# Fixing the order of the first period's loads, and regrouping the last block's output projection, in a time-mix and GELU-FFN kernel

## The chip, the cores and the metric

The kernel runs on one core of a Trainium2 chip. The metric is the device time of one execution in microseconds (us); where several runs are compared, it is their median.

## What is computed

The input x has 4 sequences of 1024 tokens with 512 channels, in float32. The reference normalizes every token over its channels and adds two branches to x:

```python
xn = _layernorm(x, axis=-1)
x = x + attn(xn) + ffn(xn)

# attn: time mix with the token before, recurrence over the tokens
xx = concatenate([x[:, 1:2, :], x[:, :-1, :]], axis=1) - x
k = einsum('btc,hc->bth', x + xx * time_mix_k, Wk)      # 704 hidden
r = einsum('btc,hc->bth', x + xx * time_mix_r, Wr)
w = exp(-exp(time_decay))
state = state * w + relu(k_t);  out_t = state * r_t     # scan over t
out = layernorm(einsum('bth,ch->btc', out, Wv)) * ln_gamma + ln_beta

# ffn: 512 -> 2048 -> 512
D = gelu(x.astype(float16) @ W0.T + bias0).astype(float16)
E = (D @ W1.T + bias1).astype(float16)
```

## The kernel before

**Blocks and periods.** The tokens are cut into 8 blocks of 512 (two for each sequence; `LAST` is 7). A block has 4 token tiles `s` of 128. The channels are 4 chunks `c` of 128, the hidden width 704 is five full tiles `h` and a half one, and the 2048 FFN units are 16 chunks `n` of 128. The main loop (L741) has one period for each block `i`, and in it one step for each FFN chunk `n` (L833).

**A step.** It issues, in this order: `up` (L654) of the chunk `AHEAD` = 2 further on, eight matmuls `pd` from W0 and the float16-rounded x; the `followers`, which are the VectorE and ScalarE work left over from the projection matmuls of the step before; the GELU of `up`'s result (L669, and a cast at L674); `down` (L679) of chunk `n`, eight matmuls for each step into four accumulators `pe`, one for each token tile; the step's entry in `pieces`, if it has one, which is a group of matmuls of the time mix (hidden tiles of k and r at the start of the period, output projection `po` at its end); and the step's list `bg[n]` of other work (loads, weight splits, normalization and transposes of the next block).

**Weights in two or three parts.** W0 and W1 are kept as high and low parts, so that their products are exact enough: `split` (L159) makes the high part on ScalarE (L160) and the low one on VectorE (L161) from a raw load. W0 stays in SBUF; its raw loads are `load_w0(g, c)` (L168), where `g` is the group of four FFN chunks that need it, and `split_w0` (L172) splits one of them. W1 is loaded raw (`load_w1_raw`, L184), split in the first period, written to DRAM (`store_weights`, L180) and fetched from there in the later periods. The weights of k and r are used raw in block 0 and in three parts from block 1 on.

**The start.** `first_inputs` (L337) normalizes, transposes on TensorE (L377, `pt`) and mixes block 0. Its x tile (`load_x`, L95) lies in a buffer of which there is one; block 1's x (`x_next`, L715) goes to the same buffer, so it can be loaded only when the last of the transposes has read block 0's. After that, L702 to L717 issue 25 loads on SyncE's queue: W0's group 0, three chunks of W1, the remaining k and r weights, the half tiles, W0's group 1, block 1's x, W0's group 2. Then a block ordered by hand (L724 to L736) computes the first hidden tiles, splits W0's group 0, splits two chunks of W1 and half of W0's group 1, and does `up` of chunks 0 and 1. In ScalarE's order the splits of W0's (1,0) and (1,1) (L735) stand ahead of the GELU of chunk 0 (L736).

**What sets the order.** A scheduler lays out each engine's instructions. Inside `tc.manual_schedule(engines=...)` the engines named keep the order of the text; elsewhere the scheduler orders by its own estimate of when things are ready. The block at L724 names TensorE, VectorE, ScalarE and SyncE; so does the first period of the main loop. The later periods name TensorE and SyncE only, so there VectorE's, ScalarE's and GpSimd's orders are the scheduler's. The loads of L702 to L717 stand in no such block.

**The end.** In the last block the last four FFN chunks (`tail` = 4) have no `down` in the loop. Their `up` runs in steps 10 to 13. The output projection stands in steps 12 to 15, one token tile each: `out_piece` (L625) issues five float32 matmuls of a tile (L588); for an odd tile it also issues the half hidden tile of both tiles of the pair (L600), and leaves as follower the residual of the pair (`residual`, L608: statistics at L265, then L615, L620, L621). The residual of tiles 2 and 3 thus comes after the loop (L866). The closing block (L868 to L880) adds a bias to two accumulators (`base`, L873), does the sixteen remaining `down` products tile by tile, and for each result rounds (L641), adds (L647) and stores (L651). The PSUM pool `mm`, with four banks, holds `pd`, `po` and the last column sums; `pe` has four banks of its own.

Of the kernel before, what the change touches and what calls it, by code (L numbers as in the profile page):

```python
# [17 lines left out]
P = 128  # L18
# [4 lines left out]
def time_mix_and_gelu_ffn(  # L23
# [26 lines left out]
    nc = tc.nc  # L50
# [4 lines left out]
    NS = TB // P  # L55
    NC = C // P
# [6 lines left out]
    NF = HID // P  # L63
    H0 = NF * P
# [3 lines left out]
    LAST = len(blocks) - 1  # L68
# [10 lines left out]
    def part(name, dtype=F32R, tag="q", bufs=QS):  # L79
        return wide.tile([P, TB], dtype, tag=tag, name=name, bufs=bufs)  # L80
# [7 lines left out]
    def bank(name):  # L88
        return ps_mm.tile([P, TB], F32, tag="mm", name=name)

    def tokens_of(i, s):
        b, t0 = blocks[i]
        return b, slice(t0 + s * P, t0 + (s + 1) * P)

    def load_x(i, name, amid=lambda: None):  # L95
        xs = const.tile([P, NS, C], F32, tag="x", name=f"{name}_{i}")
        for s in range(NS):
            if s == NS // 2:
                amid()
            b, rows = tokens_of(i, s)  # L100
            nc.sync.dma_start(xs[:, s, :], x[b, rows, :])
        return xs


    FIRST = 3
    sources = (wkT, wrT)
    raw_w = {}

    def load_raw(kind, h):
        w = part(f"w{'kr'[kind]}_{h}", F32)  # L110
        raw_w[kind, h] = w.rearrange("p (c k) -> p c k", c=NC)
        src = sources[kind].rearrange("(c p) k -> p c k", p=P)
        nc.sync.dma_start(raw_w[kind, h], src[:, :, h * P : (h + 1) * P])
# [29 lines left out]
    raw_half = part("raw_half", F32).rearrange("p (two c k) -> p two c k", two=2, c=NC)  # L143
# [24 lines left out]
    def load_w0(g, c, **home):  # L168
        w0_raw[c, g] = raw = part(f"w0raw_{g}_{c}", F32, **home)
        nc.sync.dma_start(raw, w0T[c * P : (c + 1) * P, g * TB : (g + 1) * TB])  # L170
# [13 lines left out]
    def load_w1_raw(n):  # L184
        w1_raw[n] = part(f"w1raw_{n}", F32)
        nc.sync.dma_start(w1_raw[n], w1T[n * P : (n + 1) * P, :])
# [511 lines left out]
    AHEAD = 2  # L698
    state = {}
    behind = ExitStack()  # L700
    first_x16s, pks = first_inputs(x_now, behind)
    for c in range(NC):  # L702
        load_w0(0, c)
    for n in range(AHEAD + 1):
        load_w1_raw(n)
    for h in range(FIRST, NF):
        load_raw(0, h)
        load_raw(1, h)
    for kind, src in enumerate(sources):
        nc.sync.dma_start(  # L710
            raw_half[:, kind], src.rearrange("(c p) k -> p c k", p=P)[:, :, H0:]
        )
    for c in range(NC):
        load_w0(1, c)
    x_next = load_x(1, "x")  # L715
    for c in range(NC):
        load_w0(2, c)  # L717

    def several(fn, *calls):
        for args in calls:  # L720
# [2 lines left out]
    engines = {e.engine for e in (nc.tensor, nc.vector, nc.scalar, nc.sync)}  # L723
# [15 lines left out]
    followers = []  # L739
    e16s = []  # L740
    for i in range(len(blocks)):  # L741
        with tc.manual_schedule(
            engines=engines if i == 0 else {nc.tensor.engine, nc.sync.engine}
        ):
            j = i + 1
            tail = 4 if i == LAST else 0
            by_columns = range(NS // 2, NS) if tail else ()
            pieces, bg = {}, defaultdict(list)

            def put(n, fn, *args):  # L750
                bg[n].append(lambda: fn(*args))

            def fetch_kr(block, kind, h):
                if block == 1 and kind == 1:
                    ks[block, kind, h] = split_kr(kind, h)
                else:
                    ks[block, kind, h] = load_kr(block, kind, h)

            def fetch_x():
                state["x"] = load_x(j, "x")  # L760

            def fetch_residual():
                zs[i] = load_x(i, "xres")

            def stats(*ss):
                norm_stats(j, state["x"], *ss)

            def turn(first, end):
                transposed(state["x"], first, end)

            def fresh_mixed(c):
                mixed(j, c)

            for s in range(NS):
                pieces[12 + s] = [out_piece, i, s]
            if i == 0:
                state["x"] = x_next
                pieces[1] = [raw_k, i, 3]
                pieces[3] = [raw_r, i, 3]
                pieces[5] = [raw_k, i, 4]  # L780
                pieces[7] = [raw_r, i, 4]
                pieces[9] = [
                    lambda i: raw_halves(i, [bank(f"pkr_{i}_{q}") for q in range(2)]), i
                ]
                put(0, several, split_w0, (1, 2), (1, 3))
                for c in range(NC):
                    put(2 + c - (c == 0), split_w0, 2, c)
                    put(3 + c, load_w0, 3, c)
                    put(5 + c, split_w0, 3, c)
                put(1, stats, *range(NS))  # L790
                put(3, lambda: norm_apply(j, state["x"]))
                for h in range(NF):
                    put(1 + 2 * h, split_kr, 0, h)
                put(4, turn, 0, 1)
                put(5, turn, 1, 5)
                put(7, turn, 5, 10)
                put(8, turn, 10, 11)
                put(9, turn, 11, 16)
                put(4, load_late_constants)
                put(12, split_half)  # L800
                mix_at = (11, 12, 13, 15)
            else:
                order = [(0, h) for h in range(NF)] + [(1, h) for h in range(NF)]
                for k, (kind, h) in enumerate(order):
                    pieces[k + 2 * kind] = [three_pass, i, kind, h]
                    if k > 1:
                        put(k - 2 + 2 * (k > 6), fetch_kr, i, kind, h)
                pieces[5] = [half_pass, i, 0]
                pieces[6] = [half_pass, i, 1]
                put(2, split_xr, i, 0)  # L810
                put(4, split_xr, i, 1)
                put(5, split_xr, i, 2)
                put(5, split_xr, i, 3)
                if j <= LAST:
                    put(2, fetch_x)
                    put(4, stats, *range(NS))
                    put(5, lambda: norm_apply(j, state["x"]))
                    put(6, turn, 0, 2)
                    put(7, turn, 2, 6)
                    put(8, turn, 6, 10)  # L820
                    put(9, turn, 10, 14)
                    put(10, turn, 14, 16)
                mix_at = (11, 12, 13, 14)
            put(11 if j <= LAST else 2, fetch_residual)
            if j <= LAST:
                put(10, x16, j)
                for c, n in enumerate(mix_at):
                    put(n, fresh_mixed, c)
                put(13, fetch_kr, j, 0, 0)
                put(14, fetch_kr, j, 0, 1)  # L830

            pe = [ps_e.tile([P, C], F32, tag="pe", name=f"pe_{i}_{s}") for s in range(NS)]
            for n in range(NN):  # L833
                ahead = n + AHEAD
                if ahead == NN and j <= LAST:
                    xf = ffn_input(j)
                nxt = (i, ahead) if ahead < NN else (j, ahead - NN)
                gelu = up(*nxt) if nxt[0] <= LAST else None
                for follow in followers:
                    follow()  # L840
                followers = []
                if gelu:
                    d = gelu()
                if n < NN - tail:
                    operands = waiting.pop(0)
                    for s in range(NS):
                        down(n, s, *operands, end=NN - tail if s in by_columns else NN)
                if gelu and i > 0:
                    waiting.append((d, load_w1(*nxt)))
                for s in (2 * n, 2 * n + 1):  # L850
                    if s < len(e16s):
                        finish(i - 1, s, e16s[s])
                if n in pieces:
                    fn, *args = pieces[n]
                    followers.append(fn(*args))
                if i == 0 and ahead + 1 < NN:
                    load_w1_raw(ahead + 1)
                for fn in bg[n]:
                    fn()
                if i == 0:  # L860
                    waiting.append((d, load_w1(*nxt)))
                store_weights()
            if not tail:
                e16s = [rounded(i, s, pe[s]) for s in range(NS)]
# [59 lines left out]
```

## Time and profile before

| what | value |
|---|---|
| median of 3 runs | 904.9 us (904.3 to 905.19) |
| the profiled execution | 904.43 us, its span 902.6 us |
| TensorE matmuls busy | 888.0 us (98%), 3688 instructions |
| TensorE weight loads busy | 657.7 us (73%) |
| VectorE | 590.5 us (65%) |
| ScalarE | 349.7 us (39%) |
| GpSimd | 73.1 us (8%) |
| moved by DMA | 165.60 MB, mean 183 GB/s |
| mean granted TensorE clock | 0.994 |

The profile is one execution. The span runs from the first to the last instruction of the program, and the execution's time is 1.8 us longer. Busy shares are means over stages with different limits, so the page is to be read together with the chain of waits (what released each step, followed back from the end), the list of waits by engine, the timelines, and tables of busy time by stage. A line such as `PE pe L681 <- ACT d L674` says that TensorE's matmul at line 681, which writes `pe`, waited for ScalarE's instruction at line 674, which writes `d`. In these views PE is TensorE's matmuls, PEld its weight loads, DVE VectorE, ACT ScalarE, POOL GpSimd and SP SyncE; a `q` behind an engine's name means its instruction queue, which issues DMAs. Ends of matmuls are modelled, so distances between their starts are the safer measure.

### The profile page before, as it was taken

The numbers are of one execution on the slowest core, as the hardware profiler recorded it, in microseconds if no ns is written. First come the engines' busy times: TensorE is split into PE (matmuls) and PEld (weight loads), VectorE is DVE, ScalarE is ACT, GpSimd is POOL, SyncE is SP. The second block draws the span as 40 slices with busy tenths as digits, with TensorE's granted clock in tenths as the row PEclk, the third lists the DMA queues.
The fourth block names the chain that finished last, engine by engine and source line by source line (L and its number), as shares of the span: only waits on it lengthen the run. The fifth ranks groups of instructions, "written<-read, shape, count | busy, mean of one in ns | idle before, by whom it ended". The sixth has DMA issues, their size and how long they took to land.

```text
span 902.6 us, 10591 instructions
## 1 busy us (share of the span) xinstructions
PE 888.0 (98%) x3688; PEld 657.7 (73%) x3688; DVE 590.5 (65%) x989; ACT 349.7 (39%) x597; POOL 73.1 (8%) x142
## 2 busy tenths in 40 slices
PE   8999999999999999999999999999999999999996
PEld 8577658877588866888668885788767887588854
DVE  4577886886659558595575946678555775565126
ACT  4756533554144332344324442244333444144320
POOL 1100000100111001010111000010011100000001
PEclk8999999999999999999999999999999999999999
DMA  4969746644375642945448454485535654466621
GB/s 122 323 231 331 241 163 212 220 152 143 138 240 192 198 152 94 306 156 161 147 157 275 158 190 137 142 272 162 174 120 191 237 171 144 140 220 211 190 79 47
DMA packets 77888, 165.60 MB, mean 183 GB/s; under 512 B 9199, under 2 KB 15372, under 8 KB 77836
## 3 DMA queue, kind: packets, MB, share of 16 engines
q1 hardware_dynamic: 77776, 164.92, 55.0%
q8 instruction: 29, 0.48, 0.2%
q14 instruction: 23, 0.19, 0.1%
q10 hardware_dynamic: 60, 0.02, 0.0%
HBM read 140.26 MB, written 24.64 MB: 183 GB/s over the span
## 4 chain that ended last, share of the span: by engine, by line
PE 91%; DVE 4%; DMA 2%; SPq 1%; ACT 1%; issue 1%; POOL 0%; ACTq 0%; DVEq 0%
PE pd L659 24%; PE pe L681 24%; PE po L588 15%; PE pa L534 13%; PE pb L335 7%; PE ph L562 2%; PE po L600 2%; PE pk L335 2%; DMA w0raw<-in_L_ffn_W 1%; DVE xnT L291 1%; PE pr L335 1%; DMA x<-in_L_attn_x 0%; DMA wk<-in_L_attn_Wk 0%; PE pkr L509 0%; DVE xres L647 0%
## 5 line engine op out<-in xcount | busy, mean ns | idle before, releaser
L681 PE MATMUL pe<-w,d 128*128 128x512 f32 x1008 | 249.2, 389 | 2.2 <-ACT d L674 2.2
L681 PEld LDWEIGHTS pe<-w,d 128*128 128x128 f32 x1008 | 189.0, 188 | 43.0 <-ACT d L674 2.6
L659 PE MATMUL pd<-xf,w0h 128*128 128x512 f32 x512 | 209.5, 409 | 1.3 <-DVE y L547 0.8
L659 PE MATMUL pd<-xf,w0l 128*128 128x512 f32 x512 | 199.7, 390 | 0.0
L669 ACT ACTIVATE d<-pd,late_sb 128x512 f16<-128x512 f32 x128 | 87.6, 684 | 187.0 <-PE pd L659 186.7
L588 PE MATMUL po<-wv_sb,g 128*128 128x512 f32 x320 | 142.4, 592 | 0.0
L547 DVE SCALAR_TENSOR_TENSOR y<-pb,a 128x512 f32<-128x512 f32 x70 | 48.2, 689 | 141.8 <-PE pb L335 127.0
L659 PEld LDWEIGHTS pd<-xf,w0h 128*128 128x128 f32 x512 | 96.1, 188 | 38.0 <-issue 16.1
L659 PEld LDWEIGHTS pd<-xf,w0l 128*128 128x128 f32 x512 | 96.1, 188 | 23.8 <-issue 4.5
L588 PEld LDWEIGHTS po<-wv_sb,g 128*128 128x128 f32 x320 | 60.6, 189 | 64.9 <-issue 61.8
L546 ACT ACTIVATE a<-pa 128x512 f32<-128x512 f32 x70 | 41.7, 596 | 117.2 <-PE pa L534 117.2
L674 ACT CAST d<-d 128x512 fp32r<-128x512 f16 x128 | 79.4, 621 | 3.8
L291 DVE STREAM_TRANSPOSE xnT<-x 32x512 f32<-32x512 f32 x112 | 78.7, 702 | 1.8
L265 DVE BATCH_NORM_STATS2 sty<-po 128x6 f32<-128x512 f32 x32 | 21.9, 683 | 86.2 <-PE po L600 86.2
L534 PE MATMUL pa<-hk,kr 128*128 128x512 f32 x140 | 54.5, 389 | 0.0
L534 PE MATMUL pa<-lk,kr 128*128 128x512 f32 x140 | 54.5, 389 | 0.0
L259 POOL TENSOR_SCALAR ry<-mvy 128x1 f32<-128x1 f32 x32 | 15.2, 475 | 397.2 <-DVE mvy L266 397.2
L534 PE MATMUL pa<-hr,kr 128*128 128x512 f32 x120 | 46.7, 389 | 0.0
L534 PE MATMUL pa<-lr,kr 128*128 128x512 f32 x120 | 46.7, 389 | 0.0
L549 ACT ACTIVATE y<-y 128x512 f32<-128x512 f32 x35 | 22.2, 634 | 57.3 <-DVE y L547 57.3
L246 ACT CAST hk<-uk 128x512 fp32r<-128x512 f32 x28 | 17.4, 620 | 58.4 <-DVE uk L213 58.4
L335 PE MATMUL pb<-mk,kr 128*128 128x512 f32 x140 | 37.4, 389 | 0.0
(133 smaller groups left out, 1042.3 us busy)
## 6 DMA issues: line engine op xcount, KB each, us to landing
w<-w1d SPq DMA_DIRECT2D x110, 512.0 KB, 3.5
kr<-krd SPq DMA_DIRECT2D x195, 256.0 KB, 4.1
x<-in_L_attn_x SPq DMA_DIRECT2D x32, 256.0 KB, 4.9
w1d<-w SPq DMA_DIRECT2D x16, 512.0 KB, 3.0
xres<-in_L_attn_x SPq DMA_DIRECT2D x32, 256.0 KB, 4.4
krd<-wt SPq DMA_DIRECT2D x30, 256.0 KB, 3.5
out<-xres SPq DMA_DIRECT2D x28, 256.0 KB, 4.4
w0raw<-in_L_ffn_W SPq DMA_DIRECT2D x16, 256.0 KB, 5.7
```

Source lines behind the costliest of these rows:

```text
L265: nc.vector.bn_stats(st6, src)
L291: nc.vector.transpose(dst[i * Q : (i + 1) * Q, :, :, j, :], src[j * Q : (j + 1) * Q, :, :, i, :],)
L335: return nc.tensor.matmul(dst, w[:, c, :], src, start=(c == 0), stop=(c == NC - 1))
L534: nc.tensor.matmul(pa, w[p][:, c, :], xs[j, c][p], start=(c == 0 and p == 0), stop=(c == NC - 1 and p == 1),)
L546: nc.scalar.activation(a, pa, AF.Copy, scale=1.0 + 1.0 / S)
L547: nc.vector.scalar_tensor_tensor(y, pb, -1.0 / S, a, ALU.mult, ALU.add)
L549: nc.scalar.activation(y, y, AF.Relu)
L588: nc.tensor.matmul(pos[s], gs[i, h][:, s * P : (s + 1) * P], wv_sb[:, h, :], start=(h == 0), stop=False,)
L659: nc.tensor.matmul(pd, w0[c, g][p][:, k * P : (k + 1) * P], xf[c], start=(c == 0 and p == 0), stop=(c == NC - 1 and p == 1),)
L669: nc.scalar.activation(d16, pd, AF.Gelu, bias=b0_sb[:, n : n + 1])
L674: nc.scalar.copy(d, d16)
L681: nc.tensor.matmul(pe[s] if sum_ is None else sum_, d[:, s * P : (s + 1) * P], w1[p][:, cols], start=(n == first and p == 0), stop=(n == e ...
```

## The change

There are two edits. The 25 loads of L702 to L717 are put, in the same order of the text, into a block in which SyncE keeps that order. And the entries of `pieces` are keyed by step and place (`n, s`) instead of by step, so that a step can have up to four of them; in the last block the output projection of tiles 0 and 1 is put in step 12 and that of tiles 2 and 3 in step 13, where it was one tile each in steps 12 to 15. The other blocks keep one tile for each step, and all other entries keep their steps.

```diff
-    for c in range(NC):
-        load_w0(0, c)
-    for n in range(AHEAD + 1):
-        load_w1_raw(n)
...
-    for c in range(NC):
-        load_w0(1, c)
-    x_next = load_x(1, "x")
-    for c in range(NC):
-        load_w0(2, c)
+    with tc.manual_schedule(engines={nc.sync.engine}):
+        for c in range(NC):
+            load_w0(0, c)
+        for n in range(AHEAD + 1):
+            load_w1_raw(n)
+        for h in range(FIRST, NF):
+            load_raw(0, h)
+            load_raw(1, h)
+        for kind, src in enumerate(sources):
+            nc.sync.dma_start(
+                raw_half[:, kind], src.rearrange("(c p) k -> p c k", p=P)[:, :, H0:]
+            )
+        for c in range(NC):
+            load_w0(1, c)
+        x_next = load_x(1, "x")
+        for c in range(NC):
+            load_w0(2, c)
...
             for s in range(NS):
-                pieces[12 + s] = [out_piece, i, s]
+                pieces[12 + (s // 2 if i == LAST else s), s] = [out_piece, i, s]
...
-                if n in pieces:
-                    fn, *args = pieces[n]
-                    followers.append(fn(*args))
+                for s in range(NS):
+                    if (n, s) in pieces:
+                        fn, *args = pieces[n, s]
+                        followers.append(fn(*args))
```

More of the change, by code (lines that the diff above doesn't have):

```diff
@@ L701, in time_mix_and_gelu_ffn @@
     first_x16s, pks = first_inputs(x_now, behind)
-    for c in range(NC):
-        load_w0(0, c)
-    for n in range(AHEAD + 1):
-        load_w1_raw(n)
[L706 to L712, printed above, removed]
-    for c in range(NC):
-        load_w0(1, c)
-    x_next = load_x(1, "x")
-    for c in range(NC):
-        load_w0(2, c)
+    with tc.manual_schedule(engines={nc.sync.engine}):
[15 more added lines that the diff above has]
+            load_w0(2, c)
     def several(fn, *calls):
@@ L774, in time_mix_and_gelu_ffn @@
             for s in range(NS):
-                pieces[12 + s] = [out_piece, i, s]
+                pieces[12 + (s // 2 if i == LAST else s), s] = [out_piece, i, s]
             if i == 0:
                 state["x"] = x_next
[L778 to L782, printed above, removed]
+                pieces[1, 0] = [raw_k, i, 3]
+                pieces[3, 0] = [raw_r, i, 3]
+                pieces[5, 0] = [raw_k, i, 4]
+                pieces[7, 0] = [raw_r, i, 4]
+                pieces[9, 0] = [
                     lambda i: raw_halves(i, [bank(f"pkr_{i}_{q}") for q in range(2)]), i
@@ L804, in time_mix_and_gelu_ffn @@
                 for k, (kind, h) in enumerate(order):
-                    pieces[k + 2 * kind] = [three_pass, i, kind, h]
+                    pieces[k + 2 * kind, 0] = [three_pass, i, kind, h]
                     if k > 1:
                         put(k - 2 + 2 * (k > 6), fetch_kr, i, kind, h)
-                pieces[5] = [half_pass, i, 0]
-                pieces[6] = [half_pass, i, 1]
+                pieces[5, 0] = [half_pass, i, 0]
+                pieces[6, 0] = [half_pass, i, 1]
                 put(2, split_xr, i, 0)
```

## The prediction

> **What bounds the kernel now.** I read the page's busy shares first, then TensorE's waits, then the chain of waits for 19 to 47 us, SyncE's timeline at the start, the stages, and last the end of each engine's timeline.
>
> ```profile
> PE 888.0 (98%) x3688; PEld 657.7 (73%) x3688; DVE 590.5 (65%) x989; ACT 349.7 (39%) x597; POOL 73.1 (8%) x142
> ```
>
> TensorE (PE) is busy 888.0 of 902.6 us, so only its pauses, or the stretch after its last matmul, can give time back. Its waits (total, times, longest) are few:
>
> ```profile
> PE small L410 <- issue: 2.6, 1, 2.6
> PE pe L681 <- ACT d L674: 2.2, 1, 2.2
> PE pd L659 <- DVE y L547: 0.8, 1, 0.8
> PE idle L353 <- PEq L907: 0.8, 1, 0.8
> PE pd L659 <- DVE y L573: 0.5, 1, 0.5
> ```
>
> The 2.2 us wait, `down` of chunk 0 waiting for ScalarE's (ACT's) GELU output, is the one that the first edit can reach. Followed back in the chain (start, us, what):
>
> ```profile
> 20.37 0.45 PE pt L377 x4
> ...
> 20.84 0.34 SPq L101
> ...
> 24.07 6.25 DMA w0raw<-in_L_ffn_W
> ...
> 33.28 4.97 DMA w0raw<-in_L_ffn_W
> 38.25 0.02 issue
> 38.27 0.62 ACT w0h L160
> ...
> 38.91 0.62 ACT w0h L160
> ...
> 39.55 1.28 ACT L669
> ...
> 40.84 0.70 ACT d L669
> ...
> 41.56 0.63 ACT d L674
> ...
> 42.23 2.14 PE pe L681 x8
> ```
>
> The GELU stands in ACT's queue behind the splits of `w0raw(1,0)` and `(1,1)`, which landed at 38.25. These were late because SyncE (SP) issued block 1's x first, and x waits for its single buffer, free when block 0's last transposes (L377) are over:
>
> ```profile
> 7.27 1.48 SPq L113 DMA_DIRECT2D wr<-in_L_attn_Wr  x3
> 20.84 1.76 SPq L101 DMA_DIRECT2D x<-in_L_attn_x  x4
> 22.65 1.85 SPq L170 DMA_DIRECT2D w0raw<-in_L_ffn_W  x4
> ```
>
> From 8.75 to 20.84 SP issues nothing. The stage table has the DMA engines 22% busy at 61 GB/s in 9 to 21 us, then 98% at 306 GB/s in 21 to 45.
>
> At the end VectorE (DVE) decides, from the last projection tile on:
>
> ```profile
> 887.30 0.70 DVE L265 BATCH_NORM_STATS2 sty<-po 128x6 f32<-128x512 f32 x1 [4.14 <-PE po L600]
> 892.15 0.68 DVE L873 TENSOR_TENSOR base<-pe,b_sb 128x512 f32<-128x512 f32 x1
> 899.44 0.42 DVE L647 TENSOR_TENSOR xres<-xres,e 128x256 f32<-128x256 f32 x1
> ```
>
> DVE has no further pause from 887.30 to 899.86; the last stores land at 902.6. PE's last matmul starts at 894.68, inside that.
>
> **What the Trainium skill says.** "DMA: Bandwidth & Descriptors", section "Anatomy of one DMA": DMA engines wait for no semaphore, the issuing sequencer does, before dispatch. The trace agrees: one x load holds SP for 12.0 us and the independent loads behind it start late. "Perfetto Trace Analysis", section "Tensor Engine Instruction": ACT and DVE run strictly in order, and PE's end times are estimates. The first half is what the chain shows at 38.27 (the GELU's own input was complete near 36.4); for the second I count PE's loss from starts. "ScalarE: Activation LUTs", section "What ACT_TABLE_LOAD costs", has about 1283 ns for the load; the row at 39.55 has 1.28 us.
>
> **Part 1, SP's order.** Nothing is added or removed; all 25 loads of the text keep their sizes. What moves: four x loads (0.43 us of issue each) go behind 17 others: w0(0), three w1raw, four raw weights, two half weights, w0(1). No wait is added. Behind x's wait on SP there now stand only w0(2), first split at 47.75, and the loop's loads and stores.
>
> *When does w0(1,1) land?* A 262,144-byte load at 306 GB/s takes 0.857 us. w0(1,1) is the 15th load; the halves count half each, so 14 full ones. If w0(0,0) issues at 8.8 and lands in the 5.7 us of the issue table: 8.8 + 5.7 + 13 x 0.857 = 25.6 us. The other bound: the w0 buffers could be ones that the same transposes free, so that the trace would hide their wait behind x's. Then w0(0,0) starts at 20.84 and w0(1,0) gains only x's four places: 38.25 - 4 x 0.857 = 34.8; (1,1) at about 35.5. I take the early one; it hardly matters, as follows.
>
> *What is late next?* ACT runs without a pause to the end of the w1 splits (31.57 + 1.22 = 32.79). Early bound: two splits to 34.05, table load to 35.35; then chunk 0's `up` is the later (last matmul near 36.04, over near 36.4), so GELU 36.55 to 37.25 and cast to 37.87. Late bound: splits to 36.15, table load to 37.45, GELU to 38.15, cast to 38.8. PE wants it when `up` of chunk 2 is through: last start 39.67 plus the usual 0.227 is 39.90. Both are in time, by 2.0 and 1.1 us.
>
> *Gain.* `down` begins at 39.90 instead of 42.23: 2.33. Its eight matmuls, after the pause, took 1.98 us to the next start (42.23 to 44.21) where the next group took 1.82 (46.03 to 47.85): 0.16. Together **2.5 us**. Bounds: 0 if another wait replaces all of it; not more than 2.6, since PE has no other pause there.
>
> *Does it last?* PE paces ACT, DVE and SP from 42 us on. ACT's later waits for w1raw (2.75 us at 79.37, 0.88 at 85.08) reach no PE pause; the DMA engines come out of their rush before them (66% in 45 to 67 us), and earlier w0(1) and w0(2) only thin it. DVE pauses 5.22 us before 45.47, so it carries no backlog over. x lands later: w0(1)'s last two are ahead of it, so 16 full loads, near 27.4 (8.8 + 5.7 + 15 x 0.857), then x by 31; with the late bound near 41. Its first reader in DVE's order was at 49.01, and that moves to about 46.5: covered. If it weren't, each microsecond would be one of DVE's. Early loads against the start-up: the x and wr loads are issued before, and wr is first read at 24.1. I cost that at nothing; were `products` delayed, PE would pay directly.
>
> **Part 2, the last block's projection.** Same instructions; `up` of chunk 15 (1.85 us) moves behind projection tile 1 and its halves. The chain has, on PE from 866.02: tile 0 4.29, `up` 1.85, tile 1 4.29, halves 1.02, tiles 2 and 3 8.78, halves 1.03; together 21.26, to 887.28. After it the same groups stand in another order. Only one junction differs: halves into a projection cost 0.10 (877.40 to 877.94 from start to start, where 0.43 is usual), halves into `up` 0.11 in the middle blocks (before 119.08). So nothing. Tiles 0 and 1 start their residual at about 875.6 (877.47 - 1.85) instead of 877.5, in a stretch where DVE had waited 11.77 us for it: worth nothing, since the last residual still starts when tile 3's halves end. Chunk 15's GELU comes 5.3 us later, cast done near 878.9; its first reader is beyond 888: covered by 9 us. Four PSUM banks rotate: the fourth tile needs tile 0's bank back by 881.8 and gets it near 877.8. Part 2: **0**, bounds +0.2 (junctions) and -1.2 (see the third rival).
>
> **Sum.** The profiled execution took 904.43 (span 902.6, 1.8 around it). 904.43 - 2.5 + 0 = 901.9. The median of the runs shown, 904.9, is 0.47 above that execution, so I forecast **902.4**.
>
> **Rivals.**
> *The wait moves on (0.15).* In block 1 DVE is busy for 4.4 to 5.0 of every 5 us from 165 to 195, and PE pauses twice there (0.5 and 0.8). This begins with x of block 2: its load, issued at 155.60, ends a 2.64 us wait of DVE at 160.89. If that did not come earlier with PE, the gain would melt to between 0 and 1.6: 903.3 to 904.9. Against: SP issued x right behind a weight load whose buffer PE frees. That the order does not take effect for the loads is in here, too; the late bound above says it would still gain.
> *Slower (0.11): DVE's order in block 1.* From block 1 on DVE's and ACT's order is the planner's, redrawn with its view of the first period. If the transposes (groups of 3.56 and 4.28 us at 181.26 and 187.39) came ahead of the evictions at 184.85 and 192.31, PE would pause up to 7.8 more, less the 1.25 it has: 904.9 - 2.5 + 6.6 = 909.0. Over 2.5 us of such displacement decides. For it: two pauses there show no slack. Against: all of block 1 shifts as one, which keeps the order.
> *More (0.07).* The two `base` additions (892.15 and 893.35, 1.2 us) read sums complete since 861.5. If the new place of the residuals lets DVE do them earlier, the end is 1.2 shorter: 901.2.
>
> **How the numbers follow.** Main case 0.67: 902.4, within 901.6 to 903.0, a few hundredths of it above. About 0.2% (1.8 us) is what a measurement can tell from no change: below 903.1 is faster. Faster: 0.64 of the main case and 0.07, 0.71. Within: 0.03 and 0.15, 0.18. Slower: 0.11. The range takes in the main case and the first rival, and leaves out the slower one and most of the third: 901.4 to 905.0.
>
> **What would show it.** Right: SP issues w0raw from 8.8 us, the DMA share in 9 to 21 us is above 0.7, PE's wait for `d` L674 is gone, PE starts its first `down` near 39.9, and the end looks as before, 2.5 us earlier: DVE's last pair of L265 from near 884.8. Wrong: a new PE pause before 50 us; w0raw still at 20.8; pauses at 183 to 191 above 1.3 us in all; `base` ahead of the last residual.

## The result and the profile after

| | before | after |
|---|---|---|
| median of 11 runs each | 904.52 us (903.29 to 905.84) | 902.07 us (901.21 to 903.28) |
| ratio, with its 95% interval | | 0.9973 (0.9964 to 0.9982) |
| the profiled execution | 904.43 us, span 902.6 | 901.21 us, span 899.4 |

The change makes the kernel 2.45 us faster; 2.5 were forecast, and 902.4 us. The two profiled executions lie 3.2 us apart, because that of after is the fastest of its eleven; what the other 0.7 us are is told below.

TensorE's waits, after (total us, times, longest us):

```profile
PE small L410 <- issue: 2.8, 1, 2.8
PE pd L659 <- DVE y L547: 0.8, 1, 0.8
...
PE pd L659 <- DVE y L573: 0.6, 1, 0.6
```

The line `PE pe L681 <- ACT d L674` is gone and nothing stands in its place. SyncE's timeline, after (start, length, count at the end):

```profile
7.17 1.48 SPq L113 DMA_DIRECT2D wr<-in_L_attn_Wr  x3
8.69 1.93 SPq L170 DMA_DIRECT2D w0raw<-in_L_ffn_W  x4
...
19.50 1.94 SPq L170 DMA_DIRECT2D w0raw<-in_L_ffn_W  x4
21.56 1.81 SPq L101 DMA_DIRECT2D x<-in_L_attn_x  x4
```

SyncE goes on without a long stop: W0's first loads start at 8.69 us instead of 22.65, and block 1's x at 21.56 instead of 20.84, so it hardly loses. In the table of stages for 9 to 21 us the DMA share is 1.05 by that view's count, where it was 0.22, and 309 GB/s are moved instead of 61. ScalarE's timeline after (a group's start, its length, the instruction, and in brackets the idle time before it and what ended it):

```profile
30.37 1.23 ACT L160 CAST w<-w1raw 128x512 fp32r<-128x512 f32 x2
31.41 1.23 ACT L160 CAST w0h<-w0raw 128x512 fp32r<-128x512 f32 x2
32.66 1.28 ACT L669 ACT_TABLE_LOAD   x1
35.26 0.69 ACT L669 ACTIVATE d<-pd,late_sb 128x512 f16<-128x512 f32 x1 [1.32 <-PE pd L659]
35.98 0.62 ACT L674 CAST d<-d 128x512 fp32r<-128x512 f16 x1
```

The splits of W0's (1,0) and (1,1) wait for no load any more, and the GELU waits for its own matmuls, as the step "what is late next" had it. Its cast is done at 36.60, and the first `down` starts at 38.69: 15.78 us after the first `pr` matmul (L335), where it was 18.12, and where the 39.9 of the forecast makes 15.79. At the end VectorE does the same things in the same order. One line of before, then after's:

```profile
877.50 0.70 DVE L265 BATCH_NORM_STATS2 sty<-po 128x6 f32<-128x512 f32 x1 [11.77 <-PE po L600]
```

```profile
872.43 0.70 DVE L265 BATCH_NORM_STATS2 sty<-po 128x6 f32<-128x512 f32 x1 [9.92 <-PE po L600]
...
884.08 0.70 DVE L265 BATCH_NORM_STATS2 sty<-po 128x6 f32<-128x512 f32 x1 [5.98 <-PE po L600]
...
888.92 0.68 DVE L875 TENSOR_TENSOR base<-pe,b_sb 128x512 f32<-128x512 f32 x1
...
896.21 0.43 DVE L647 TENSOR_TENSOR xres<-xres,e 128x256 f32<-128x256 f32 x1
```

The first residual waits 9.92 us instead of 11.77, the second 5.98 instead of 4.14: the 1.85 us won by the regrouping are waited off again before the second.

**Where the time went.** Four marks on TensorE cut every profiled execution: the first `pr` matmul (L335), the 41st `down` matmul (L681), the first projection matmul (L588) of the last block, the end of the span. Starts alone are used, but for that end. The rows below the second are the kernels of the experiments further down; each has one profile.

| kernel | start to first pr | to 41st down | to last block's projection | to the end |
|---|---|---|---|---|
| before | 24.11 | 43.33 | 798.42 | 36.78 |
| after | 22.91 | 40.81 | 798.92 | 36.80 |
| loads alone | 23.68 | 40.81 | 798.00 | 36.79 |
| projection alone | 24.23 | 42.48 | 800.08 | 36.80 |
| x first | 23.31 | 44.64 | 798.28 | 36.79 |
| x after group 0 | 23.53 | 40.81 | 798.55 | 36.79 |
| GELU first | 24.34 | 43.15 | 799.37 | 36.79 |
| GELU and stores first | 23.61 | 40.80 | 798.54 | 36.80 |
| all four tiles in a step | 24.67 | 40.81 | 799.80 | 34.94 |
| base early | 24.47 | 40.80 | 797.74 | 35.48 |
| both of these | 24.61 | 40.81 | 798.65 | 33.87 |

The second column holds the whole effect of the change, 2.52 us; the fourth shows that the regrouped projection is worth 0.0. The first differs between kernels with the same work there, and the third although the order of work in that stretch is the same (see "Does it last" below). That is the rest of the 3.2 us: 1.20 less at the start, 0.5 more in the middle.

### The profile page after: what moved, and what is told of

It reads as the page before. It is cut to its first block, busy times and chain, and to the rows that moved or that the text cites. A ratio compares the mean times of both kernels' runs of the same rounds, so it can differ in the third digit from the quotient of the medians.

```text
span 899.4 us, 10592 instructions
## 1 busy us (share of the span) xinstructions
PE 886.8 (99%) x3688; PEld 656.7 (73%) x3688; DVE 590.6 (66%) x989; ACT 349.1 (39%) x597; POOL 72.7 (8%) x142
## 4 chain that ended last, share of the span: by engine, by line
PE 94%; DVE 4%; issue 1%; DMA 1%; POOL 0%; ACT 0%; SPq 0%; DVEq 0%
PE pd L659 25%; PE pe L681 24%; PE po L588 15%; PE pa L534 13%; PE pb L335 7%; PE ph L562 2%; PE pk L335 2%; PE pr L335 2%; PE po L600 2%; DVE xnT L291 1%; DMA x<-in_L_attn_x 1%; PE idle L353 1%; PE pkr L509 0%; DVE xres L647 0%; DVE stx L265 0%
## 5 line engine op out<-in xcount | busy, mean ns | idle before, releaser
L681 PE MATMUL pe<-w,d 128*128 128x512 f32 x1008 | 249.3, 389 | 0.0
L681 PEld LDWEIGHTS pe<-w,d 128*128 128x128 f32 x1008 | 189.1, 188 | 40.7 <-issue 0.8
L588 PE MATMUL po<-wv_sb,g 128*128 128x512 f32 x320 | 142.2, 592 | 0.0
L588 PEld LDWEIGHTS po<-wv_sb,g 128*128 128x128 f32 x320 | 60.6, 190 | 64.5 <-issue 62.0
L674 ACT CAST d<-d 128x512 fp32r<-128x512 f16 x128 | 79.4, 620 | 3.9
L335 PE MATMUL pb<-mk,kr 128*128 128x512 f32 x140 | 37.4, 389 | 0.0
```

What stands on the lines that cost most here:

```text
L335: return nc.tensor.matmul(dst, w[:, c, :], src, start=(c == 0), stop=(c == NC - 1))
L588: nc.tensor.matmul(pos[s], gs[i, h][:, s * P : (s + 1) * P], wv_sb[:, h, :], start=(h == 0), stop=False,)
L674: nc.scalar.copy(d, d16)
L681: nc.tensor.matmul(pe[s] if sum_ is None else sum_, d[:, s * P : (s + 1) * P], w1[p][:, cols], start=(n == first and p == 0), stop=(n == e ...
```

## Experiments

Theory: all of the gain is TensorE's pause before the first `down`, which late W0 loads cause through ScalarE's queue. Rivals: the projection has a share; a new plan for the later periods does it; late loads cost in further ways. Each time is a median of several rounds against the kernel before on the same chip.

**1. Each edit alone.** The changed kernel with its `pieces` of before, and with its loads of before:

```diff
-                pieces[12 + (s // 2 if i == LAST else s), s] = [out_piece, i, s]
+                pieces[12 + s, s] = [out_piece, i, s]
```

```diff
-    with tc.manual_schedule(engines={nc.sync.engine}):
-        for c in range(NC):
-            load_w0(0, c)
+    for c in range(NC):
+        load_w0(0, c)
...
```

> The loads in the fixed order, the last block's projection as before. Theory (all of the gain is TensorE's pause before the first down, which early W0 loads remove): 2.5 us less than before, ratio 0.9973, TensorE's wait for d L674 gone, the tail from the last residual's first statistics to the end still 15.3 us. Rival (the regrouped projection carries a share): at most half of it, above 0.998.

> The regrouped projection alone, the loads in the scheduler's order. Theory: 0.0 +- 0.3 us against before, ratio 1.000; the wait of 2.2 us for d L674 stays, and tiles 0 and 1 begin their residual 1.9 us earlier with nothing following from it. Rival (the projection carries a share of the 2.45 us): 1 us or more less than before.

Measured: loads alone 901.48 us against 904.43, ratio 0.9961 (0.9949 to 0.9974); projection alone 904.69 us, ratio 1.0000 (0.9992 to 1.0008). The projection has no share. With it alone the pause for `d` of L674 is there, but only 1.4 us long, because in that execution W0's (1,0) was split at 37.51 instead of 38.27; its 41st `down` is 1.67 us behind the changed kernel's. A further 0.5 us of wait for a W1 low part of L161 comes at 89.02, behind that mark.

**2. x put first in the fixed order.**

```diff
     with tc.manual_schedule(engines={nc.sync.engine}):
+        x_next = load_x(1, "x")
         for c in range(NC):
             load_w0(0, c)
...
-        x_next = load_x(1, "x")
```

> Both edits, but in the hand-ordered block the second block's x stands first, where the scheduler had put it. Theory (x's place does it, not the fact that the order is fixed): the pause of 2.2 us is back, SyncE sits until 20.8 us, time as before within 0.3 us, ratio 1.000. Rival (another plan for all later periods does it): still 2 us or more less than before.

Measured: 905.24 us against 904.43, ratio 1.0006 (0.9998 to 1.0014). SyncE sits until 20.04 us, and TensorE waits 1.9 us for `d` L674. So x's place does it; that the order is fixed does nothing by itself.

**3. x right behind W0's group 0.** The same edit, with x after the first `load_w0` loop.

> Both edits, but x stands right behind the four loads of W0's group 0, so that W1, the raw k and r weights and W0's group 1 wait behind it. This gives the prediction's late bound: W0's (1,0) lands near 34.8 us instead of 38.25. Theory (only what lands later than ScalarE and TensorE can use costs, and 1.1 us are left): no pause before the first down, 2.5 us less than before, ratio 0.9973. Rival (every microsecond by which these loads come later is paid): the gain shrinks to about 1 to 1.5 us, with a pause of 1 us or more.

Measured: 901.47 us against 904.43, ratio 0.9962 (0.9948 to 0.9975). ScalarE's timeline of this run:

```profile
33.55 1.29 ACT L160 CAST w0h<-w0raw 128x512 fp32r<-128x512 f32 x2 [1.33 <-DMA w0raw<-in_L_ffn_W]
34.86 1.28 ACT L669 ACT_TABLE_LOAD   x1
36.16 0.69 ACT L669 ACTIVATE d<-pd,late_sb 128x512 f16<-128x512 f32 x1
```

W0's (1,0) lands at 33.5 us, ScalarE waits 1.33 us for it, and TensorE pays nothing for that: 40.81 us to the 41st `down`, as with the early loads. In the changed kernel these loads are issued 9.4 us sooner (19.50 against 28.93), and that brings nothing more.

**4. The loads late, the GELUs ahead of the splits.** In the kernel before only ScalarE's order changes:

```diff
-        several(split_w0, (1, 0), (1, 1))
         waiting = [(up(0, n)(), w1s[n]) for n in range(AHEAD)]
+        several(split_w0, (1, 0), (1, 1))
```

> The kernel before, loads and projection untouched; only ScalarE's hand-written order is changed: the GELUs of chunks 0 and 1 stand ahead of the splits of W0's (1,0) and (1,1) instead of behind them. The loads stay late (38 us). Theory (the late loads cost only through this queue, the GELU behind a split that waits): TensorE's wait for d L674 is gone and the time falls by 2.5 us as with the early loads, ratio 0.9973. Rival (the late loads cost in other ways too, say by the DMA engines' rush or by x and W0's second group): less than 1.5 us of gain, or a new pause between 40 and 60 us.

Measured: 905.06 us against 904.71, ratio 1.0001 (0.9989 to 1.0013). The theory missed here. The wait for `d` L674 is gone, the first `down` starts at 40.09, and yet the 41st `down` comes 43.15 us after the first `pr`. TensorE's, SyncE's and ScalarE's timelines of this run, and last ScalarE's of the kernel before:

```profile
56.11 0.50 PE L681 MATMUL pe<-w,d 128*128 128x512 f32 x1 [1.53 <-ACT w L160]
56.84 1.90 PE L681 MATMUL pe<-w,d 128*128 128x512 f32 x7 [0.22 <-DVE w L161]
```

```profile
33.61 4.62 SPq L170 DMA_DIRECT2D w0raw<-in_L_ffn_W  x8
...
39.26 9.98 SPq L182 DMA_DIRECT2D w1d<-w  x3
```

```profile
47.55 0.62 ACT L160 CAST w<-w1raw 128x512 fp32r<-128x512 f32 x1 [4.44 <-DMA w1d<-w]
```

```profile
45.99 0.62 ACT L160 CAST w<-w1raw 128x512 fp32r<-128x512 f32 x1
```

The pause has moved. Split W1 chunks have two buffers (`tag="w1"`, L194), so chunk 2's split waits until the store of chunk 0 has landed. That store is issued at 39.26, behind eight late W0 loads and a raw W1 load, and lands at 47.45. ScalarE waits 4.44 us. VectorE and ScalarE, in order behind it, are late with chunk 3's parts, for which TensorE waits at 56.11 and 56.84. By starts, `down` of chunks 0 to 2 is on time, and that of chunk 4 is 2.35 us behind the changed kernel's. (One more wait for a W1 low part, 1.0 us, comes at 90.28, behind the mark.) In the kernel before the store lands at 45.89, and the same split starts 0.1 us later with no wait shown: ScalarE got to it only then, since the late W0 loads had held it before. With x first (experiment 2), where the pause is 1.9 us, the same split waits 0.43 us for the store. So the late loads had two prices, one behind the other. The second theory: only a kernel in which the store gets away early, too, gains the 2.5 us.

**5. The stores ahead of W0's group 2, too.**

```diff
-    for c in range(NC):
-        load_w0(2, c)
...
         waiting = [(up(0, n)(), w1s[n]) for n in range(AHEAD)]
+        several(split_w0, (1, 0), (1, 1))
+        store_weights()
+        for c in range(NC):
+            load_w0(2, c)
```

> As the run with the GELUs ahead of the splits, with one more edit: the four loads of W0's group 2 are issued behind the first stores of split W1 chunks instead of ahead of them; x and all other loads stay as late as before. Theory (in that run the pause did not go away but moved: the split of W1's chunk 2 needs the buffer of chunk 0, whose store stood behind eight late W0 loads and landed at 47.4 us): the store lands about 3.4 us sooner (four loads of 0.857 us), the new pauses go, 2.5 us less than before, ratio 0.9973. Rival (late loads cost for another reason): still 1.000.

Measured: 901.53 us against 904.45, ratio 0.9972 (0.9960 to 0.9983), with x still ahead of W0. SyncE's and ScalarE's timelines:

```profile
34.82 1.05 SPq L182 DMA_DIRECT2D w1d<-w  x2
36.61 3.08 SPq L170 DMA_DIRECT2D w0raw<-in_L_ffn_W  x4
```

```profile
42.30 0.62 ACT L160 CAST w<-w1raw 128x512 fp32r<-128x512 f32 x1
```

The split starts at 42.30 without a wait, TensorE has no pause there, and the mark is at 40.80. With both prices taken away the gain of the change is there, with x and W0's groups 0 and 1 as late as before: the theory is shown from the other side. The early store alone, with the GELUs still behind the splits, was not run. The store was issued 4.4 us sooner (34.82 against 39.26) and landed at 41.33 instead of 47.45; counted from the first `pr` that is 5.4 us sooner, where 3.4 were expected. The raw W1 load behind W0's group 2 had also stood ahead of it, which makes 4.3 (five loads of 0.857 us); the rest stays open.

**6. What the end is bound by.** Three versions of the changed kernel: all four tiles in step 12; the `base` additions in step 12 of the last block in other buffers; both.

```diff
-                pieces[12 + (s // 2 if i == LAST else s), s] = [out_piece, i, s]
+                pieces[12 + (0 if i == LAST else s), s] = [out_piece, i, s]
```

```diff
+                if tail and n == NN - tail:
+                    for s in by_columns:
+                        bases[s] = part(f"base_{s}", F32)
+                        nc.vector.tensor_add(bases[s], pe[s], b1_sb)
...
-        for s in by_columns:
-            bases[s] = temp(f"base_{s}")
-            nc.vector.tensor_add(bases[s], pe[s], b1_sb)
```

> The changed kernel with all four projection tiles of the last block in step 12, so that up of chunk 15 (1.85 us) stands behind them. Theory (the end is VectorE's queue of 12.3 us from the end of the last projection tile on, so only TensorE work that is moved behind that tile counts, and the two-tile grouping moves none): 1.8 us less than the changed kernel, about 4.4 us less than before, ratio 0.995; at most 0.2 us of a new wait for chunk 15's GELU. Rival (the end is bound by TensorE or by the stores): as the changed kernel, ratio 0.997.

> The changed kernel with the two base additions of the end written into step 12 of the last block, in buffers of another pool tag, so that they need not follow the residual's temporaries. Theory (VectorE's queue sets the end): 1.2 us less than the changed kernel, about 3.8 us less than before, ratio 0.996. Rival: as the changed kernel, ratio 0.997.

> All four tiles in step 12 and the early base additions together. Theory: the two add up, 3.0 us less than the changed kernel, 5.6 us less than before, ratio 0.994; TensorE's last matmul then starts about 3.5 us ahead of VectorE's last addition, less than the 4.7 us of before. Rival (a floor set by TensorE's last products or by the stores): no more than 2 us less than the changed kernel.

Measured against 904.71: all four 899.98, ratio 0.9950 (0.9936 to 0.9964); base early 901.03, 0.9955 (0.9942 to 0.9969); both 899.11, 0.9938 (0.9924 to 0.9952). By the last column of the table the end is 1.86, 1.32 and 2.93 us shorter than after's. They nearly add up, and the last version beats both kernels. TensorE's and VectorE's timelines of it:

```profile
882.55 1.09 PE L600 MATMUL po<-wv_sb,gh 64*64 64x512 f32 x8
885.52 4.24 PE L681 MATMUL pe<-w,d 128*128 128x512 f32 x16
```

```profile
883.67 0.70 DVE L265 BATCH_NORM_STATS2 sty<-po 128x6 f32<-128x512 f32 x1 [4.14 <-PE po L600]
...
889.24 0.68 DVE L641 TENSOR_TENSOR e<-pe,b_sb 128x512 f16<-128x512 f32 x1
...
894.73 0.43 DVE L647 TENSOR_TENSOR xres<-xres,e 128x256 f32<-128x256 f32 x1
```

Between the halves and `down` now stands `up` of chunk 15, and VectorE's queue is 11.5 us long instead of 12.6, with no `base` in it. TensorE's last matmul starts at 893.30, 1.4 us ahead of VectorE's last addition. I had expected 3.5. That was a slip of mine in the sum: both edits pull VectorE's end towards a TensorE end that stays, so from the 4.76 us of before it had to be 4.8 - 3.0 = 1.8, less 0.3 for the slower `down` group (4.24 us instead of 3.93).

## Why the prediction was right, point by point

- **The pause and its chain: right.** 2.33 + 0.16 = 2.49 us were counted from the starts; the marks give 2.35 to the first `down` and 2.52 to the 41st, the medians 2.45. That it fits so closely is luck: the interval of the ratio takes in gains from 1.6 to 3.3 us, and the forecast took the size of the pause from one execution (2.2 us), where other profiles with the same late loads and the same order on ScalarE have 1.4 and 1.9.
- **When the loads land: right in kind.** The w0 buffers waited for nothing. Of W0's group 1 the first load landed at 23.68 and the last at 26.46, around the 25.6 counted for (1,1), and the splits found their data. Experiment 3 comes near the late bound without being the same kernel: 33.5 us, where 34.8 were counted, and as foreseen it cost TensorE nothing.
- **"Not more than 2.6, since PE has no other pause there": right for this change, for a reason it did not see.** The view of pauses shows only the wait that ended last. Behind it stood a second wait that the first had just covered, W1's buffers (experiment 4). The prediction's list of what is late next had only the GELU's inputs in it. That the gain was not eaten up there is luck as far as the prediction goes: the earlier loads free SyncE's queue and the DMA engines as well, so that the first store is issued at 32.77 instead of 38.95, and it has landed at 35.38, long before the split at 41.23.
- **Does it last: right.** PE's pauses in block 1 are 0.56 and 0.82 instead of 0.47 and 0.78 us. Together that is 1.38, a little above the 1.3 that the prediction had named as a sign of being wrong; but it is 0.13 more than before, and the gain did not melt there. The rival in which VectorE's order is redrawn did not come: in the traces VectorE, ScalarE and GpSimd do the same instructions in the same order in both kernels (compared by tile names without buffer numbers), on SyncE only the four loads of x have another place, and on TensorE only `up` of chunk 15. So a new plan for the later periods is no cause of the gain either.
- **The projection: right.** 0.0, and the end 36.80 us long instead of 36.78. The third rival's mechanism is real (`base`, 1.2 us foreseen, 1.32 found), but the change does not set it off: in after, `base` stands where it stood, at the end of the last residual.
- **The number.** 902.4 against 902.07; the median of before is 904.52 over eleven runs and not 904.9, which is more than the difference.

## What to carry to other kernels

In an in-order issue queue a load that must wait for a buffer belongs behind the loads that need not; but only so far forward as somebody waits for the data, for here issuing W0's group 1 another 9.4 us sooner than in experiment 3 bought nothing. A pause shows only the wait that ended last: before an edit is credited with it, look for waits that end within the pause's length of it, above all buffers freed by stores that stand in the same queue. And where one engine's queue sets the end, as VectorE's does here, what counts is that it starts sooner, by moving other engines' work behind its last input (1.86 us), or that it gets shorter (1.32 us); regrouping on another engine that leaves the last input where it was is worth nothing.

## What the runs showed of the hardware

The granted clock of TensorE at the start differs between profiled executions: half speed for 6.8 us (7.28 to 14.10) in before, for 3.4 us (7.97 to 11.38) in after. It goes with the column "start to first pr": 24.1 to 24.7 us in the five profiles with 6.8 us, 22.9 to 23.7 in the five with 3.4. Both groups hold kernels with the same work there, so the edits do not set it; whether the chip or the moment does was not tested. In the eleventh (projection alone) the record begins only at 13.4 us. A profile's span can thus be 1.2 us off for no reason of the kernel's, which is why only distances between marks are compared above.

In the run with x first a second such stretch came 1.5 us after the pause, from 42.69 to 46.10. Busy time by stage there (us, length, then PE, PEld, DVE, ACT, POOL, clock, DMA):

```profile
39.00:42.70 3.70, 1.78 (x9) 1.26 (x8) 0.20 (x1) 3.56 (x6) 0.00 (x0) 1.00 0.96 339
42.70:46.10 3.40, 3.40 (x10) 2.63 (x9) 1.40 (x3) 2.79 (x5) 0.00 (x0) 0.50 0.75 301
```

TensorE has 10 matmuls in those 3.4 us where the kernel before, between the same times, had 17. From `down` of chunk 0 to that of chunk 1 it took 5.38 us instead of 3.80; that is the 44.64 in the table against 43.33. Whether the pause set this off is not shown: it is one of four profiles with the late loads and a pause of 1.4 to 2.2 us, and the other three have no such stretch. Whether it explains why the ratios of experiments 1 and 3 came out at 0.996 rather than 0.997 stays open.

The third column moves by up to 2.3 us, and this can be placed, though not explained. Against the kernel before, the step from `down` of chunk 9 to that of chunk 10 in the first period takes up to 1.3 us more (the waits at 89.02 and 90.28 named above are in it), block 1 from 0.7 less to 0.5 more, blocks 2 and 3 up to 0.7 more. From block 4 to the last block's projection all eleven profiles agree within 0.1 us. With one profile for each kernel it can't be said whether the kernel or the execution makes these differences.
